# Last part of a Perceiver block on one core: tile 0's steps set between tile 1's, roots by ScalarE's table, and a causal mask added by TensorE

## The chip, the core and the metric

The kernel runs on one core of a Trainium2 chip. A core has TensorE (matrix products into PSUM), VectorE, ScalarE (elementwise functions from a loaded table) and GpSimd, and queues that start DMAs (SyncE's, called SP below, and ScalarE's own). The profile calls them PE (PEld for its weight loads), DVE, ACT, POOL and SP. PSUM has eight banks of 128 x 512 f32. The metric is the device time of one execution, in microseconds; a measurement is the median of several runs.

## What is computed

Everything is float32. Four batches of 256 tokens of width 256 go through three layers; the context of each batch is 4096 tokens of width 192.

```python
x1 = x + xattn(layernorm(x), ctx)      # 16 heads of 16, softmax over 4096 context tokens
x2 = x1 + attn(layernorm(x1))          # causal; q and k normed per head, then scaled
x  = x2 + ffn(layernorm(x2))           # 64 slots: routing, gates, slot attention
# ffn: logits = gelu([x, slot_mean] @ w1 + b1) @ w2 + b2, over |tau| + 0.1
#      alpha  = softmax over the 8 largest of 64, else 0
#      slots  = GRU(alpha^T x / sum alpha, slot_init); slots attend to each other; layernorm
#      out    = alpha @ (slots @ wvp + bvp) @ wo + bo
```

## The kernel before

**The main loop.** For every batch, pairs of 128 context tokens are taken in 16 steps: scores (L165), exp on ScalarE (L1778, L1780), products with the values (L179), sums kept in SBUF by VectorE (L1794). What follows the cross attention of batch b (its output, self attention and feed forward) is cut into small steps, and a dictionary places them between the steps of batch b+1. On TensorE, VectorE and ScalarE the instructions stand in the order in which the program issues them (`manual_schedule`); a step that waits holds all that is behind it on its engine.

**The last batch.** Nothing follows batch 3, so its 256 queries are split into two tiles of 128 (t = 0, 1) at the end: tile 0's cross attention is finished first, and `tile_out` and `tile_in` (L2133, L2156) take tile 0 up to its scaled q and k while tile 1's last context tokens are still being scored. `ending` (L2174) does the rest: both tiles' self attention, the feed forward of batches 2 and 3 together (`both_`, 64 slots each), and the output of all four batches. The eight banks are named x_0, x_1, y_0, y_1, z_0, z_1, w_0, w_1, in pairs x_, y, z, w. Temporaries come from a ring of eight buffers (`temp`).

Names that the prediction uses:

- `tile_qk`, `tile_heads`, `tile_factors` (L1987, L2015, L2021): q and k of a tile in one product, their squares (ScalarE, `Square`), the sum of squares per head (VectorE, L2017), and q and k scaled by one over the root (L2022). `tile_in` finds that root on VectorE alone: `rsqrt` (L925) with a first guess and three Newton rounds of three instructions (L935 to L941). In `ending`, tile 1 uses ScalarE's Sqrt (L2227, L2232) and a reciprocal.
- `preload` (L944) runs a function on one element, so that ScalarE loads its table there.
- `tile_qk_turned` (L2029): q and k transposed by TensorE and moved with gain and bias.
- `first_scores`, `first_weigh` (L2060, L2080): tile 0's queries against tile 0's keys, 16 heads in eight products, exp, and the products with the values. A product of 32 rows uses one of four row strips of TensorE; which one is set by `pair_rows(h, m)`.
- `second_scores`, `second_exp`, `second_mask`, `second_weigh` (L2094 to L2114): the same for tile 1's queries against both tiles' keys, for c = 0, 1 and h = 0, 1; the mask multiplies the part of tile 1's own keys by the triangle `tri` (`tile_mask`, L2053).
- `fill` (L1055): products of zeros into an unused bank, 0.43 us each by its constant.
- `project`, `residual`, `tile_stats`, `normed`: output projection onto the residual in PSUM, its mean and variance, and the normed rows x2n.
- `chosen` (L1433): routing; the largest eight logits, two exps on ScalarE (L1446), alpha (L1448 to L1452). `slot_inputs` (L1456), `gates` (L1494), `slot_qk`, `slot_scores`, `slot_v`, `at_turned`, `mixed_channels_first` (L1600), `slot_values`: the slots' part.
- `given_out` (L1660): the output of one batch, two products with the identity that bring in x2, two with alpha, a copy by ScalarE, and a DMA on SP. Before, batch 0's stands behind the gates, batch 1's behind `at_turned`; batches 2 and 3 are sent last, one on SP and one on ScalarE's queue.

## Time and profile before

| | us |
|---|---|
| median of 3 runs | 851.98 (850.6 to 852.13) |
| the profiled execution | 850.88 |
| its span (first to last instruction) | 849.1 |
| `ending` starts (last products with the context's values, L1900) | 786.2 |
| last product of TensorE ends | 842.07 |
| last two output DMAs are issued | 842.76 and 842.93 |

The page's busy table gives each engine's time at work and its share of the span; the table by stage does the same for stretches of the span. The chain of waits is followed back from the last instruction: at each step to what released it. In the timeline a row is start, length, engine, line, operation, output and inputs, count, and in brackets how long the engine had been idle and who ended that. A product in f32 stands as two records, a transpose as one. Between the last product and the end of the span lie 7 us: the last copies, their DMAs, and the program's end.

### The profile page before, as it was taken

What the parts mean: (1) busy time and instruction counts of PE and PEld (TensorE: products, weight loads), DVE (VectorE), ACT (ScalarE), POOL (GpSimd) and SP (SyncE); (2) the same over time, 40 slices, a digit from 0 to 9 for tenths busy, and PEclk for the clock granted to TensorE, in tenths of its full rate; (3) what the DMA queues carried; (4) which work ended last, traced back from release to release, by engine and by line L of the source; (5) the groups of instructions that cost most, each with busy time, mean ns of one, the idle gap of its engine ahead of it and who ended that gap; (6) DMA issues with size and microseconds to landing.
All of it is one profiled execution on the core that took longest, in us unless ns stands there. A gap on an engine that the chain in (4) does not pass through costs nothing.

```text
span 849.1 us, 19377 instructions
## 1 busy us (share of the span) xinstructions
PE 826.4 (97%) x8403; PEld 451.4 (53%) x8403; DVE 307.3 (36%) x776; ACT 606.0 (71%) x841; POOL 16.8 (2%) x20
## 2 busy tenths in 40 slices
PE   8999999999999999999999999999999999999886
PEld 5445555545555545545545555554545554567564
DVE  3123234222263353212253353232344442113654
ACT  5776776767677768777778777766778777777542
POOL 1000100000000010000000010000000000000000
PEclk9999999999999999999999999999999999999999
DMA  7601001000000000000000000000000000000001
GB/s 205 138 27 50 26 22 55 27 26 25 26 26 26 2 26 26 26 25 27 27 25 26 2 26 26 26 25 10 19 25 26 27 25 25 2 3 2 2 1 54
DMA packets 21822, 25.86 MB, mean 30 GB/s; under 512 B 6241, under 2 KB 13281, under 8 KB 21729
## 3 DMA queue, kind: packets, MB, share of 16 engines
q1 hardware_dynamic: 20784, 23.75, 9.6%
q8 instruction: 68, 1.11, 0.5%
q10 hardware_dynamic: 848, 0.79, 0.3%
q14 instruction: 26, 0.21, 0.1%
q0 software_dynamic: 96, 0.01, 0.0%
HBM read 23.48 MB, written 1.05 MB: 29 GB/s over the span
## 4 chain that ended last, share of the span: by engine, by line
PE 93%; DVE 3%; ACT 2%; issue 1%; DVEq 0%; ACTq 0%
PE banks L165 28%; PE banks L179 25%; PE banks L993 7%; PE banks L80 7%; PE banks L107 7%; PE banks L86 4%; PE banks L120 4%; PE banks L1876 2%; PE banks L1900 1%; PE banks L981 1%; PE banks L1843 1%; PE banks L1058 1%; PE banks L1812 1%; PE banks L194 1%; ACT prob L1780 1%; PE banks L1461 1%
## 5 line engine op out<-in xcount | busy, mean ns | idle before, releaser
L1780 ACT ACTIVATE prob<-banks 128x1024 f32<-128x1024 f32 x360 | 343.8, 1043 | 0.0
L165 PE MATMUL banks<-qh,kt 32*128 32x512 f32 x1920 | 250.2, 620 | 1.2 <-DVE qh L1036 1.2
L179 PE MATMUL banks<-prob,v 128*32 128x256 f32 x3840 | 219.6, 381 | 0.8 <-ACT prob L1822 0.5
L1778 ACT ACTIVATE prob<-banks 128x512 f32<-128x512 f32 x240 | 130.3, 595 | 121.7 <-PE banks L165 121.4
L179 PEld LDWEIGHTS banks<-prob,v 128*32 128x32 f32 x3840 | 118.6, 110 | 117.0 <-ACT prob L1778 42.8
L165 PEld LDWEIGHTS banks<-qh,kt 32*128 32x128 f32 x1920 | 97.6, 183 | 111.1 <-issue 62.5
L1794 DVE TENSOR_TENSOR sums<-banks,sums 128x512 f32<-128x512 f32 x112 | 77.1, 691 | 178.4 <-PE banks L179 155.8
L107 PE MATMUL banks<-wv,ctx 128*128 128x256 f32 x256 | 61.6, 384 | 0.0
L80 PE MATMUL banks<-ctx,wk 128*128 128x512 f32 x128 | 61.5, 603 | 0.1
L107 PEld LDWEIGHTS banks<-wv,ctx 128*128 128x128 f32 x256 | 46.8, 190 | 14.2 <-ACT prob L1778 6.8
L150 DVE COPY v<-banks 128x512 f32<-128x512 f32 x35 | 23.9, 691 | 81.6 <-PE banks L120 77.2
L94 DVE TENSOR_SCALAR kt<-banks,bk 128x512 f32<-128x512 f32 x32 | 24.0, 751 | 66.9 <-PE banks L86 66.8
L150 ACT COPY v<-banks 128x512 f32<-128x512 f32 x29 | 17.0, 587 | 30.0 <-PE banks L120 28.8
L120 PE MATMUL banks<-wv,ctx 64*128 64x256 f32 x256 | 36.3, 402 | 0.0
L86 PE MATMUL banks<-ctx,wk 64*128 64x512 f32 x128 | 36.1, 641 | 0.0
L95 ACT ACTIVATE kt<-banks,bk 128x512 f32<-128x512 f32 x32 | 22.1, 690 | 17.9 <-PE banks L86 17.1
L80 PEld LDWEIGHTS banks<-ctx,wk 128*128 128x128 f32 x128 | 20.9, 189 | 21.2 <-ACT prob L1780 12.1
L120 PEld LDWEIGHTS banks<-wv,ctx 64*128 64x128 f32 x256 | 22.0, 186 | 11.1 <-issue 9.3
L1822 ACT ACTIVATE prob<-banks 128x512 f32<-128x512 f32 (+1 forms) x30 | 17.9, 693 | 8.5 <-PE banks L1812 8.5
L987 DVE COPY tmp<-banks 128x512 f32<-128x512 f32 x17 | 11.8, 691 | 32.8 <-PE banks L981 32.8
L1890 ACT ACTIVATE prob<-banks 128x1024 f32<-128x1024 f32 x24 | 22.9, 1043 | 0.0
L993 PE MATMUL banks<-wqkv,tmp 128*128 128x256 f32 (+1 forms) x56 | 19.6, 482 | 0.5 <-ACT prob L1822 0.5
(310 smaller groups left out, 601.4 us busy)
## 6 DMA issues: line engine op xcount, KB each, us to landing
ctx<-in_ctxT SPq DMA_DIRECT2D x32, 256.0 KB, 3.0
ctx<-in_ctxT SPq DMA_DIRECT2D x64, 128.0 KB, 3.2
x<-in_x SPq DMA_DIRECT2D x4, 256.0 KB, 3.3
wih<-in_ffn_WihT SPq DMA_DIRECT2D x1, 768.0 KB, 7.1
tmp<-in_ffn_WhhT SPq DMA_DIRECT2D x3, 256.0 KB, 4.1
out<-tmp SPq DMA_DIRECT2D x3, 256.0 KB, 2.4
wq<-in_L_xattn_Wq ACTq DMA_DIRECT2D x1, 256.0 KB, 5.6
wo<-in_L_xattn_Wo SPq DMA_DIRECT2D x1, 256.0 KB, 4.7
```

The costliest lines, as they stand in the source:

```text
L80: nc.tensor.matmul(pk[c], k.wk[:, 0, c * P : (c + 1) * P], cx[:, 0, :], start=True, stop=False)
L86: nc.tensor.matmul(pk[c], k.wk[left(c), 1, c * P : (c + 1) * P], cx[left(c), 1, :], start=False, stop=True,)
L94: nc.vector.tensor_scalar(kt[:, 0, :], pk[0], k.bk[:, 0:1], None, ALU.add)
L107: nc.tensor.matmul(pv[n // 2][:, n % 2, :], cx[:, 0, n * P : (n + 1) * P], k.wv[:, 0, :], start=(n % 2 == 0), stop=False, skip_group_check ...
L120: nc.tensor.matmul(pv[u][:, i, :], cx[left(u), 1, n * P : (n + 1) * P], k.wv[left(u), 1, :], start=False, stop=True, skip_group_check=True,)
L150: copy(v[:, :, 0 : H * VW].rearrange("p i (h w) -> p i h w", w=VW)[:, :, :, 0:D], src.rearrange("p i (h d) -> p i h d", d=D),)
L165: nc.tensor.matmul(sc[:, m, :], kt[r, c, i * P : (i + 1) * P], qh[r, c, :], start=True, stop=True)
L179: nc.tensor.matmul(po[q * 32 : (q + 1) * 32, s * NQ : (s + 1) * NQ], v[:, i, w0 : w0 + 32], pr[s][:, m, e * NQ : (e + 1) * NQ], start=(fir ...
L993: nc.tensor.matmul(dst, lhs(c), rhs(c), start=(c == 0), stop=(c == 1))
L1778: nc.scalar.activation(pt[:, m, :], sc[:, m, :], AF.Exp)
L1780: nc.scalar.activation(pt, sc, AF.Exp)
L1794: nc.vector.tensor_tensor(s.sums[c], bank, s.sums[c], ALU.add)
```

## The change

- **Set-up**: a second constant, `hidden_by`, is made from the triangle `tri`: 0 where a key is visible, -2^100 where it is hidden.
- **`tile_in`**: alpha's transposes go to another bank and their copy later; the root of tile 0 is taken as tile 1's (`tile_roots`: ScalarE's Sqrt, then a reciprocal), with an Exp preload behind it.
- **`ending`, first half**: tile 0's transposes, moves, first scores, exps and weighing are cut by half (`tile_turned`, `tile_moved`, `first_scores(s, pair, c, h)`, `first_weigh(s, pr, g, bank)`) and set between tile 1's steps. The second scores are issued by (c, h), own keys first. In two of the four cases (bank pair y) TensorE first writes `ident @ hidden_by` into the part of the own keys, and the scores are added to it; these have no multiplication by VectorE. The other two keep theirs.
- **`ending`, second half**: the fills are gone; `tile_stats` and the roots come in another order; Gelu, Exp and Sqrt are preloaded; `given_out` is split into `residual_out` (the two products that bring in x2) and the rest; batch 0's output goes ahead of the routing's exps and batch 1's ahead of `slot_qk`.

Helpers not shown are the old ones cut in two (`tile_stats` and `tile_variance` return their second half, `tile_weigh` takes the blocks it is to do, `tile_v` the halves). The core of the diff:

```diff
@@ -1139,6 +1141,9 @@
         nc.vector.tensor_scalar(tri, bank[:, 0:P], 0.0, None, ALU.is_ge)
+        nc.vector.tensor_scalar(
+            hidden_by, tri, 2.0**100, -(2.0**100), ALU.mult, ALU.add
+        )
         for v in vself:
...
+        var = s.var_t[:, t, :]
+        rs = small.tile([P, 2 * H + 1], F32, name="rs_t", tag="rs_t", bufs=1)
+        nc.scalar.activation(rs[:, 2 * H :], var[:, 2 * H :], AF.Sqrt)
         nc.vector.tensor_reduce(
-            s.var_t[:, t, 0 : 2 * H], sq.rearrange("p (h d) -> p h d", d=D), AX.X, ALU.add
-        )
+            var[:, 0 : 2 * H], sq.rearrange("p (h d) -> p h d", d=D), AX.X, ALU.add
+        )
+        nc.vector.tensor_scalar(var[:, 0 : 2 * H], var[:, 0 : 2 * H], BIG, None, ALU.min)
+        nc.scalar.activation(
+            rs[:, 0 : 2 * H],
+            var[:, 0 : 2 * H],
+            AF.Sqrt,
+            bias=s.eps_t[:, t : t + 1],
+            scale=1.0 / D,
+        )
+        return rs
...
-    def first_scores(s, pairs):
-        prs = []
+    def first_scores(s, pair, c, h):
+        for m in range(2):
+            r = pair_rows(h, m)
+            nc.tensor.matmul(
+                pair[:, m, c * NQ : (c + 1) * NQ],
+                s.sk[r, c, 0:P],
...
+    def second_hidden(pair):
         for m in range(2):
             nc.tensor.matmul(
+                pair[:, m, NQ : 2 * NQ],
+                ident,
+                hidden_by.unsqueeze(1).to_broadcast([P, 2, P]),
                 start=True,
+                stop=False,
+                skip_group_check=True,
+            )
+    def second_scores(s, c, h, pair, add=False):
+        for j in (1, 0):
+            for m in range(2):
+                r = pair_rows(h, m)
+                nc.tensor.matmul(
+                    pair[:, m, j * NQ : (j + 1) * NQ],
+                    s.sk[r, c, j * P : (j + 1) * P],
+                    s.sq[r, c, :, P:],
+                    start=not (add and j == 1),
+                    stop=True,
+                    skip_group_check=add,
+                )
...
@@ -2158,18 +2199,18 @@
         s, d = batches[B - 1], batches[B - 2]
         s.x1T = halves(temp())
         tokens_turned(x_0, s.xo, 0)
+        move = alpha_turned(d, x_1, True)
         tokens(s.x1T, x_0, 0, nc.vector.tensor_copy)
-        alpha_turned(d, y_1)
         s.qk = held.tile([P, QT, 2 * C], F32, name="qk", tag="qk", bufs=1)
         s.sq = held.tile([P, 2, 2, NQ], F32, name="sq", tag="sq", bufs=1)
         s.sk = held.tile([P, 2, NQ], F32, name="sk", tag="sk", bufs=1)
-        sq = tile_qk(s, 0, x_1)
+        sq = tile_qk(s, 0, x_0)
         tile_v(s, 0, y_0)
-        tile_heads(s, 0, sq)
-        heads_ = s.var_t[:, 0, 0 : 2 * H]
-        nc.vector.tensor_scalar(heads_, heads_, 1.0 / D, s.eps_t[:, 0:1], ALU.mult, ALU.add)
-        s.rs0 = rsqrt(s.var_t[:, 0, :])
-        tile_factors(s, 0, x_1, s.rs0[:, 0 : 2 * H])
+        move()
+        s.rs0 = tile_roots(s, 0, sq)
+        preload(AF.Exp)
+        nc.vector.reciprocal(s.rs0, s.rs0)
+        tile_factors(s, 0, x_0, s.rs0[:, 0 : 2 * H])
...
         tile_add(s, 0, y_1, 1)
-        tile_weigh(blocks, 1, x_0)
-        tile_add(s, 1, x_0, 1)
-        tile_qk_turned(s, 0, z_0, z_1, act, act, act)
-        tile_v_moved(s, 0, y_0, s.rs0[:, 2 * H :])
-        for c, bank in enumerate((w_0, w_1)):
-            tile_turn(tile_of(s.sums[c], 1), bank)
+        tile_weigh(blocks, 1, x_1, (0,))
+        tile_turned(s, 0, 0, z_0)
+        tile_weigh(blocks, 1, x_1, (1,))
+        tile_add(s, 1, x_1, 1)
+        for i in range(2):
+            tile_moved(s, 0, i, z_0, act)
+        tile_turn(tile_of(s.sums[0], 1), w_0)
+        tile_turned(s, 0, 1, z_1)
+        tile_moved(s, 0, 4, z_1, act)
+        tile_turn(tile_of(s.sums[1], 1), w_1)
         puts = [tile_divide(s, bank, (c,), 0, 1) for c, bank in enumerate((w_0, w_1))]
         tokens_turned(y_1, s.att, 1)
         tokens(s.attT, y_1, 1, vec.tensor_copy)
         for put in puts:
             put(vec.tensor_copy)
-        prs = first_scores(s, (z, w))
+        tile_v_moved(s, 0, y_0, s.rs0[:, 2 * H :])
+        first_scores(s, z, 0, 0)
+        first_scores(s, z, 1, 0)
+        f0 = second_exp(z)
         project(s, wo, x_0, 1)
         tile_residual(s, x_0, 1)
+        first_scores(s, w, 0, 1)
+        tokens_turned(y_1, s.xo, 1)
+        var = tile_variance(s, 1)
+        tokens(s.x1T, y_1, 1, vec.tensor_copy)
+        var()
+        first_scores(s, w, 1, 1)
+        f1 = second_exp(w)
         preload(AF.Sqrt)
-        tokens_turned(y_1, s.xo, 1)
-        tokens(s.x1T, y_1, 1, vec.tensor_copy)
-        tile_mask(prs[0].rearrange("p m (u q) -> p m u q", q=P))
-        tile_variance(s, 1)
         sq = tile_qk(s, 1, x_1)
-        tile_mask(prs[1].rearrange("p m (u q) -> p m u q", q=P))
-        tile_v(s, 1, x_0)
-        var = s.var_t[:, 1, :]
-        rs = small.tile([P, 2 * H + 1], F32, name="rs_t", tag="rs_t", bufs=1)
-        act.activation(rs[:, 2 * H :], var[:, 2 * H :], AF.Sqrt)
-        tile_heads(s, 1, sq)
-        nc.vector.tensor_scalar(
-            var[:, 0 : 2 * H], var[:, 0 : 2 * H], BIG, None, ALU.min
-        )
-        act.activation(
-            rs[:, 0 : 2 * H], var[:, 0 : 2 * H], AF.Sqrt, bias=s.eps_t[:, 1:2], scale=1.0 / D
-        )
-        nc.vector.reciprocal(rs, rs)
+        for pt in (f0, f1):
+            tile_mask(pt.rearrange("p m (u q) -> p m u q", q=P))
+        first_weigh(s, f0, 0, z_0)
+        tile_v(s, 1, x_0, (0,))
+        first_weigh(s, f1, 1, z_0)
+        tile_v(s, 1, x_0, (1,))
+        rs = tile_roots(s, 1, sq)
+        sums0 = op.tile([P, 2 * NQ], F32, name="sums", tag="sums")
+        vec.tensor_copy(sums0[:, 0:C], z_0[:, 0:C])
+        act.copy(sums0[:, C:], z_0[:, C:])
+        sums0 = sums0.rearrange("p (g q) -> p g q", q=P)
+        preload(AF.Exp)
+        vec.reciprocal(rs, rs)
         tile_factors(s, 1, x_1, rs[:, 0 : 2 * H])
-        first_weigh(s, prs, z_0)
-        sums0 = as_sums(z_0, 4, act.copy)
-        preload(AF.Exp)
+        second_hidden(y)
         for c in range(2):
             tile_turn(sums0[:, 2 * c : 2 * c + 2, :], z_1, c)
-        fill(w_0, 0.86)
-        tile_qk_turned(s, 1, y_0, y_1, vec, vec, act)
+        for i, bank in enumerate((w_0, w_1)):
+            tile_turned(s, 1, i, bank)
+        tile_moved(s, 1, 0, w_0, vec)
+        tile_moved(s, 1, 1, w_0, vec)
+        tile_moved(s, 1, 4, w_1, act)
         tile_v_moved(s, 1, x_0, rs[:, 2 * H :])
         s.att, s.attT = halves(temp()), halves(temp())
         put = tile_divide(s, z_1, (0, 1), 1, 0)
         put(vec.tensor_copy)
-        for j in range(2):
-            for h, pair in enumerate((x_, y)):
-                second_scores(s, 0, h, pair, j)
-        p0 = [second_exp(pair) for pair in (x_, y)]
-        tokens_turned(w_0, s.att, 0)
         with_abo(0)
-        tokens(s.attT, w_0, 0, vec.tensor_copy)
-        residual(0, w_1)
-        second_mask(p0[0])
-        p1 = []
-        for h, pair in enumerate((x_, y)):
-            for j in range(2):
-                second_scores(s, 1, h, pair, j)
-            p1.append(second_exp(pair))
-        project(s, awo, w_1, 0, alone=False)
-        second_mask(p0[1])
-        mv0 = tile_stats(w_1[:, 0:C])
+        second_scores(s, 0, 0, y, True)
+        p00 = second_exp(y)
+        second_scores(s, 0, 1, w)
+        p01 = second_exp(w)
+        tokens_turned(x_1, s.att, 0)
+        tokens(s.attT, x_1, 0, vec.tensor_copy)
+        with_abo(1)
+        residual(0, x_0)
+        second_scores(s, 1, 0, z)
+        p10 = second_exp(z)
+        second_hidden(y)
+        second_scores(s, 1, 1, y, True)
+        p11 = second_exp(y)
+        preload(AF.Sqrt)
+        second_mask(p01)
+        second_weigh(s, p00, 0, 0, w_0)
+        second_weigh(s, p01, 0, 1, w_0)
+        second_mask(p10)
+        sums0 = as_sums(w_0, 2, vec.tensor_copy)
+        project(s, awo, x_0, 0, (0,), alone=False)
+        second_weigh(s, p10, 1, 0, w_1)
+        second_weigh(s, p11, 1, 1, w_1)
+        tile_turn(sums0, z_0)
+        sums1 = as_sums(w_1, 2, vec.tensor_copy)
+        residual(1, w_0)
+        put0 = tile_divide(s, z_0, (0,), 1, 1)
+        tile_turn(sums1, z_1)
+        project(s, awo, x_0, 0, (1,), alone=False)
+        tokens_turned(y_0, s.att, 1, (0,))
+        tokens(s.attT, y_0, 1, act.copy, (0,))
+        put1 = tile_divide(s, z_1, (1,), 1, 1)
+        tokens_turned(y_1, s.att, 1, (1,))
+        mv0 = tile_stats(x_0[:, 0:C])
+        tokens(s.attT, y_1, 1, act.copy, (1,))
+        project(s, awo, w_0, 1, alone=False)
         rs2 = small.tile([P, 2], F32, name="rs2_t", tag="rs2_t", bufs=1)
-        nc.vector.tensor_scalar(rs2[:, 0:1], mv0[:, 1:2], EPS, BIG, ALU.add, ALU.min)
-        with_abo(1)
-        second_weigh(s, p0, 0, z_0)
-        sums0 = as_sums(z_0, 2, vec.tensor_copy)
-        second_mask(p1[0])
-        preload(AF.Sqrt)
-        residual(1, w_0)
-        act.activation(rs2[:, 0:1], rs2[:, 0:1], AF.Sqrt)
-        second_mask(p1[1])
-        second_weigh(s, p1, 1, z_1)
-        sums1 = as_sums(z_1, 2, vec.tensor_copy)
-        tile_turn(sums0, x_0)
-        put0 = tile_divide(s, x_0, (0,), 1, 1)
-        tile_turn(sums1, y_0)
-        tokens_turned(x_1, s.att, 1, (0,))
-        tokens(s.attT, x_1, 1, act.copy, (0,))
-        put1 = tile_divide(s, y_0, (1,), 1, 1)
-        tokens_turned(y_1, s.att, 1, (1,))
-        project(s, awo, w_0, 1, (0,), alone=False)
-        tokens(s.attT, y_1, 1, act.copy, (1,))
-        nc.vector.reciprocal(rs2[:, 0:1], rs2[:, 0:1])
...
+        def root(t, mv):
+            nc.vector.tensor_scalar(rs2[:, t : t + 1], mv[:, 1:2], EPS, BIG, ALU.add, ALU.min)
+            act.activation(rs2[:, t : t + 1], rs2[:, t : t + 1], AF.Sqrt)
+            nc.vector.reciprocal(rs2[:, t : t + 1], rs2[:, t : t + 1])
...
-        normed(0, w_1, mv0)
-        project(s, awo, w_0, 1, (1,), alone=False)
-        act.copy(s.x2[:, 0, :], w_1[:, 0:C])
+        root(0, mv0)
+        normed(0, x_0, mv0)
         mv1 = tile_stats(w_0[:, 0:C])
+        root(1, mv1)
...
+        tokens_turned(x_1, s.x2n, 0)
+        tokens(s.x2nT, x_1, 0, act.copy)
+        residual_out(batches[0], y_0)
         normed(1, w_0, mv1)
...
-        gelu0 = hidden_product(0, x_1)
-        fill(y_1, 0.43)
-        tokens_turned(z_1, s.x2n, 1)
+        gelu0 = hidden_product(0, w_1)
+        tokens_turned(z_0, s.x2n, 1)
+        preload(AF.Gelu)
         gelu0()
-        tokens(s.x2nT, z_1, 1, vec.tensor_copy)
+        tokens(s.x2nT, z_0, 1, vec.tensor_copy)
+        logits(s, 0, x_1[:, 0:SLOTS])
+        gelu1 = hidden_product(1, z_1)
+        gelu1()
+        preload(AF.Exp)
+        act.copy(s.x2[:, 0, :], x_0[:, 0:C])
         act.copy(s.x2[:, 1, :], w_0[:, 0:C])
-        hidden_product(1, w_1)()
-        with_bias(s, "x2", s.x2, fbo)
         put0(vec.tensor_copy)
         put1(vec.tensor_copy)
-        logits(s, 0, x_0[:, 0:SLOTS])
-        fill(y_1, 0.43)
-        logits(s, 1, y_0[:, 0:SLOTS])
         lg = small.tile([P, QT, SLOTS], F32, name="lg", tag="lg", bufs=1)
-        for t, bank in enumerate((x_0, y_0)):
+        logits(s, 1, y_1[:, 0:SLOTS])
+        for t, bank in enumerate((x_1, y_1)):
             nc.vector.tensor_tensor(lg[:, t, :], bank[:, 0:SLOTS], b2, ALU.add)
         route = chosen(s, lg)
         next(route)
-        slot_inputs(d, z_0, z_1)
-        fill(x_1, 0.86)
+        slot_inputs(d, w_1, z_0)
+        given_out(batches[0], y_0)
         finish(route)
-        slot_inputs(s, y_1, w_0)
-        alpha_turned(s, w_1)
-        finish(gates(both_, x_1, z_1, y_0))
+        with_bias(s, "x2", s.x2, fbo)
+        slot_inputs(s, z_1, x_1)
+        alpha_turned(s, w_0)
+        finish(gates(both_, w_1, z_0, y_1))
         check_range = all_in_range()
         next(check_range)
-        given_out(batches[0], x_0)
-        slot_qk(both_, y_1, w_0)()
-        mixing = slot_scores(both_, w_1)
+        residual_out(batches[1], x_0)
+        given_out(batches[1], x_0)
+        slot_qk(both_, z_1, x_1)()
+        mixing = slot_scores(both_, w_0)
...
-        move = slot_v(both_, x_1)
+        move = slot_v(both_, y_0)
         finish(mixing)
+        preload(AF.Sqrt)
         move()
-        kept_slots(both_, z_1)
-        at_turned(both_, y_1)
...
-        for t in range(QT):
-            nc.tensor.matmul(
-                w_1[:, t * C : (t + 1) * C], ident, d.x2[:, t, :], start=(t == 0), stop=False,
+        residual_out(d, x_1)
...
```

## Prediction

> **What bounds the kernel now.** The page's busy table and 40 slices come first, then the table by stage, with columns start:stop, length, then busy time (and count) of TensorE, its weight loads, VectorE, ScalarE and GpSimd, granted clock, DMA share, GB/s.

> ```profile
> span 849.1 us, 19377 instructions
> PE 826.4 (97%) x8403; PEld 451.4 (53%) x8403; DVE 307.3 (36%) x776; ACT 606.0 (71%) x841; POOL 16.8 (2%) x20
> ...
> 790.00:800.00 10.00, 8.36 (x52) 4.80 (x56) 6.29 (x19) 5.96 (x10) 0.00 (x0) 1.00 0.00 0
> 800.00:810.00 10.00, 7.89 (x84) 5.48 (x86) 5.57 (x14) 7.18 (x11) 0.00 (x0) 1.00 0.01 2
> 810.00:820.00 10.00, 7.51 (x91) 4.78 (x84) 6.54 (x22) 4.76 (x11) 0.51 (x1) 1.00 0.01 2
> ```

> Up to some 780 us TensorE is never idle, and the change leaves that order alone. What can move is the last 65 us, where no engine is full and the end hangs on a chain of handovers. So I read the chain of waits (start, length, what held it) from 785 us on:

> ```profile
> 789.35 0.70 DVE qk L2022
> ...
> 798.70 1.13 DVE prob L2053
> ...
> 802.18 0.86 PE banks L1058 x4
> ...
> 811.42 1.21 DVE prob L2053 x2
> ...
> 835.81 0.87 PE banks L1664 x4
> 836.67 1.06 PE banks L1646 x4
> ```

> Here stand the things the change touches: the factors of tile 0 (L2022), which end ten small VectorE steps of a root (L935 to L941); masks L2053; `fill` products L1058; the output of batch 1 (L1664, L1646) ahead of the slots' mixing.

> The timeline gives the prices:

> ```profile
> 804.51 1.15 PE L2098 MATMUL banks<-sq,sk 32*128 32x256 f32 x16 [1.02 <-DVE rect L1934]
> 807.68 0.73 PEld L2098 LDWEIGHTS banks<-sq,sk 32*128 32x128 f32 x8 [0.18 <-ACT prob L2108]
> 795.75 1.28 ACT L946 ACT_TABLE_LOAD   x1
> 797.04 0.20 ACT L946 ACTIVATE preload<-ones 1x1 f32<-1x1 f32 x1
> 831.33 0.59 ACT L1670 COPY tmp<-banks 128x512 f32<-128x512 f32 x1 [0.80 <-PE banks L1646]
> 837.78 0.71 PE L1600 MATMUL banks<-atT,fv 128*128 128x128 f32 x4
> ```

> One product is two records. Sixteen records over four row strips take 1.15 us; eight that use only two strips still load for 0.73 us, as long as the sixteen (0.74 at 804.50). So scores issued by one half (h) alone run two at a time: 0.85 us for four products.

> **The sum.** I laid the new order out engine by engine: each step starts at its engine's previous end or, if later, 0.03 us (0.05 on TensorE) after what it waits for, with durations from these rows. Below, "old" is the trace, and differences are new minus old.

> *Tile 0's roots.* Old: `alpha_turned` writes y_1 and waits until 782.78 for an exp that reads that pair; the q,k product follows at 783.41. New: it writes x_1, free at 781.86, so q,k starts at 782.50 and the Square is held only by the last exp (784.61): it ends at 785.22, not 786.03. Then, new on ScalarE: alphaT's copy 0.37, a table load 1.28, two roots 0.20 and 0.32, to 787.35 (VectorE's reduce 0.68 and min 0.19 lie beside). Reciprocal 0.36, factors 0.69: 788.46 against 790.04. The ten steps removed took 787.06 to 789.32. Little of this 1.6 reaches the end at once: three quarters of the weighing must pass TensorE first (to 788), the last quarter follows, so the second turning of sums starts only 0.5 earlier and the tokens are copied at 792.3 against 792.83. The added Exp load (1.28) and preload (0.20) lie beside the transposes; uncovered they would cost 1.5.

> *Projection of tile 1.* Old: after all eight `first_scores` products, which also waited for the dens copies: end 795.21. New: only four go before (0.85 instead of 1.79 from the same point): 0.5 + 0.9 gives -1.4. Residual, transposes, tokens and q,k keep this lead (q,k ends 797.3 against 798.67).

> *Roots of tile 1.* Square waits for the Sqrt preload at 797.7, not TensorE, and keeps -1.0; but both masks (2 x 1.22) now precede the reduce instead of holding it (798.70 in the chain), and the factors end at 800.6 against 802.13: -1.5. The q,k transposes no longer stand behind two fill products (0.86): scores can start at 802.25 against 804.51, -2.25.

> *Second scores and masks.* Two mask summands of two products each are added: 4 x 0.43 = 1.7 us of TensorE. The first pair lies beside the roots. The second waits for the exp of the bank (804.5) and is on the path: with two-strip scores the last exp ends at 808.55 against 809.88, so 0.9 of the lead is given back. But its bank now needs no mask: old, VectorE had statistics, a bias add, a copy and two masks (2 x 0.65) after it, and the weighing ended at 813.08; new, the weighing follows that exp directly and ends at 810.0: -3.1. Division, projection, statistics, root and norm (same rows) keep -3.0: 815.0 against 817.99.

> *Routing.* The Gelu preload holds logits 0 until 816.2, and these hold the second hidden product: -2.8 at the logits (818.45 against 821.27). Then a wait is added. On ScalarE the two exps of the routing now stand behind `given_out` of batch 0, whose copy (0.59) waits for `slot_inputs` (1.5) and two 64-row products (1.13) on TensorE: 820.5. The exps end at 821.7; VectorE, done with the other inputs at 820.3, waits 1.4, and behind it alpha, the inputs and the gates. Lead here: -1.45, kept to snT (830.4 against 831.97).

> *Mixing.* L1600 stood behind batch 1's output, 835.64 to 837.73, while atT was ready at 836.14: 1.6 lost. The output now goes before `slot_qk`, beside the gates. Lead -3.3, and -3.4 at the last product (838.7 against 842.07).

> The DMAs of batches 0 and 1 go out earlier on SP (old 831.94 and 838.4), each landing some 2.4 us later with nothing else in that queue; the last two are unchanged. GpSimd's bias add starts at 819.6 as before (819.49), with 19 us to spare. The new VectorE step that makes the mask (128x128; nearest row L1141, 0.28) lies in the first 70 us.

> Laying out the *old* order in the same way ends 0.5 us before its trace, nearly all in the last 15 us, so I take like with like: -3.0. Bounds come from the price of changing the shape of products on TensorE, which no row isolates: at 0 the difference is -3.5, at 0.2 us it is -2.1; I take 0.1, which fits the old trace best. The profiled execution was 850.88 (span 849.1), giving 847.9. That is 1.1 below the median of the runs, 851.98, so the forecast against the median is 849.0.

> [...] The table-load rows show the next instruction 0.01 us after 1.28: no more. [...]

> For the clock:

> ```profile
> 844.00:845.00 1.00, 0.00 (x0) 0.00 (x0) 0.00 (x0) 0.00 (x0) 0.00 (x0) 1.00 0.97 323
> 845.00:846.00 1.00, 0.00 (x0) 0.00 (x0) 0.00 (x0) 0.00 (x0) 0.00 (x0) 0.55 0.36 122
> 846.00:847.00 1.00, 0.00 (x0) 0.00 (x0) 0.00 (x0) 0.00 (x0) 0.00 (x0) 0.50 0.10 25
> ```

> The clock halves 3.0 us after the last product. The change removes every fill in this part, and my layout has one gap of 2.4 us (820.5 to 822.9); the old order's longest is 1.2. [...]

> **Rivals.**
> *The lead is eaten on the way (about 851, no change).* ScalarE now carries two more loads and more waits; if the wait before the routing's exps is 1 us longer and the two-strip scores 1 us dearer, -1.0 remains: 851.0. For: -1.45 is all that is left at the gates in my sum. Against: the -1.9 after it is a removed queue, not a race.
> *The clock halves in the 2.4 us gap (slower, about 855.5).* After it the chain holds 6.6 us of products (0.66 inputs, 1.2 gates, 1.1 and 0.33 of q,k and scores, 0.33, 0.71, 1.13, 1.14). Half speed to the end costs +6.6: 849.0 + 6.6 = 855.6; one stretch as long as the 3.4 us up to the first gates costs 2 and ends within no change. It is slower from 4.7 us of doubled products on. For: 3.0 us of idleness did it, and nothing fills the gaps any more. Against: 2.4 is less.
> *More is won (847.3).* If the exps get through before batch 0's output, the 1.4 returns; only the written order of ScalarE speaks against it, firmly.

> **Numbers.** Forecast 0.64, eaten 0.18, clock 0.12, more 0.06. 0.2% (1.7 us) is what a measurement here can tell: faster is below 850.3. The forecast's own bounds (-3.5 to -2.1, and 1 us of spread between runs) are 847.5 to 850.9, mostly faster: with "more", 0.66. Same: 0.22. Slower: 0.12. The range reaches down for "more" and up through "eaten" to 852.8, leaving out most of the clock.

> **What would show it.** In the new profile: factors of tile 0 some 1.6 earlier; last second exp to weighing with no VectorE between; ScalarE's copy for batch 0's output just ahead of the routing's exps, with VectorE idle about 1.4 before L1453; TensorE idle 2.4 there, clock 1.00; L1606 directly after atT. A clock of 0.5 before the last product, or table loads that hold the next instruction longer than 1.3, would make it wrong.

## The result and the profile after

| | before | changed |
|---|---|---|
| median of 4 runs | 851.64 us (850.60 to 852.13) | 4627.69 us (4624.19 to 4629.42) |
| ratio | | 5.434, 95% interval 5.425 to 5.444 |
| span of the profiled execution | 849.1 | 4627.6 |
| instructions in it | 19377 | 47480 |
| the four outputs are all issued by | 842.93 | 845.11 |

The kernel takes five times as long, and not in the part that was changed. The page of the changed kernel, its first lines and two of its costliest groups (group, count, then busy time and mean ns):

```profile
span 4627.6 us, 47480 instructions
PE 3430.5 (74%) x18909; PEld 1338.5 (29%) x18909; DVE 3585.2 (77%) x3999; ACT 1836.0 (40%) x2308; POOL 161.3 (3%) x94
...
L406 ACT ACTIVATE gprob<-gprob 128x1024 f32<-128x1024 f32 x512 | 540.7, 1057 | 679.2 <-DVE gprob L403 507.1
L378 DVE TENSOR_TENSOR top<-top,raw 128x1024 f32<-128x1024 f32 x512 | 623.6, 1218 | 70.9 <-ACT raw L377 70.9
```

L362 to L406 do not run at all in the kernel before. They belong to `exact`, a second path that stands in both kernels and that no line of the diff touches. Behind the outputs stands a test: `all_in_range` compares every softmax denominator kept in the tile `dens` with 1e-10 and 1e15, `count_bad` counts the rows that fail, and a branch runs `exact` if there is one:

```python
    redo = fast(tc, a, out, k, const, x0)
    with tc.If(redo > 0):
        exact(tc, a, out, k)
```

The chain of waits of the changed kernel (start, length, what held it) shows the branch being taken:

```profile
844.39 0.70 DVE tmp L2437
845.55 0.82 ACTq L2543
846.65 6.22 DMA g_x<-in_x
...
881.33 1.23 DVE top L378
882.55 1.13 DVE ne L379
```

L2437 is the last step of the output, L2543 hands the count of the test to the queues, and right behind it x is loaded again as `g_x`. From there to the end all four batches are computed a second time.

What made the test fail is in the timeline of the changed kernel. `dens` gets batch 3's self-attention denominators by two small copies, L1955 (`put0` and `put1`, which `tile_divide` returns):

```profile
816.62 0.41 PE L1959 MATMUL banks<-ident,x2n 128*128 128x128 f32 x2
817.06 0.42 DVE L1965 COPY tmp<-banks 128x256 f32<-128x256 f32 x1 [0.53 <-PE banks L1959]
817.41 0.15 DVE L1955 COPY dens<-banks 128x8 f32<-128x8 f32 x1
...
818.11 0.66 PE L993 MATMUL banks<-tmp,w 128*128 128x128 f32 x4
...
819.21 0.17 DVE L1955 COPY dens<-banks 128x8 f32<-128x8 f32 x1 [1.65 <-ACT hT L2372]
```

The trace calls every bank `banks`; the code says which. `put0` reads z_0 and `put1` reads z_1. In the new order `tokens_turned(z_0, s.x2n, 1)` writes z_0 at 816.62 and `hidden_product(1, z_1)` writes z_1 at 818.11, both ahead of the copies. The trace even puts the second copy's wait down to ScalarE's Gelu (L2372), which reads that hidden product and has nothing to do with denominators. So `dens` holds elements of x2n and of the hidden layer. No view shows the values; a row of x2n has mean zero, so some should be negative, below the test's 1e-10. Before, put0 and put1 read x_0 and y_0, which nothing writes until the logits (L1417), and these come behind both copies:

```profile
819.26 0.23 DVE L1942 COPY dens<-banks 128x8 f32<-128x8 f32 x2
...
819.95 0.33 PE L1417 MATMUL banks<-w,hT 128*128 128x64 f32 x2
```

In the part that was changed, the outputs are 2.2 us later than before too, where the forecast had them 3 us earlier. Of these 2.2, 1.04 had come up in the main loop of that execution; 1.1 are left. The same chain there:

```profile
806.65 1.06 PE banks L2124 x4
...
822.10 0.59 ACT tmp L1682
822.68 0.49 ACT tmp L1451 x2
824.39 2.82 PE banks L1466 x12
```

The second mask summand (L2124) holds the last scores; the copy of batch 0's output (L1682) holds the routing's exps (L1451); and the second slot inputs (L1466) take 2.82 us, against 1.55 at full clock (824.10 to 825.65 in the kernel gap_filled, below). VectorE's wait for the exps (L1453) and TensorE's gap behind it stand in the timeline:

```profile
823.20 0.29 DVE L1453 SCALAR_TENSOR_TENSOR lg<-tmp 128x128 f32<-128x128 f32 x1 [1.31 <-ACT tmp L1451]
...
824.39 1.12 PE L1466 MATMUL banks<-alpha,sumto 128*128 128x64 f32 x4 [2.33 <-DVE alpha L1457]
```

The table by stage (start:stop, length, busy us of TensorE, its loads, VectorE, ScalarE, GpSimd, clock, DMA share, GB/s) shows the clock of these slow products:

```profile
816.28:819.69 3.41, 2.14 (x16) 1.72 (x16) 1.05 (x5) 2.35 (x5) 0.00 (x0) 1.00 0.00 0
819.69:823.11 3.42, 2.37 (x16) 1.84 (x15) 2.01 (x11) 2.52 (x7) 1.26 (x1) 1.00 0.00 0
823.11:826.52 3.41, 2.13 (x10) 2.13 (x11) 1.82 (x6) 0.06 (x1) 0.00 (x0) 0.50 0.21 77
```

The granted clock is 0.50 from 823.11 to 829.93 and again from 836.76 to 840.17, for 6.83 and 3.41 us. The first fall comes 1.05 us into TensorE's gap of 2.33 (822.06 to 824.39), not behind it.

### The profile page after: what moved, and what is told of

Same layout as the page of the kernel before. It is cut to its first block, busy times and chain, and to the rows that moved or that the text cites. A ratio compares the mean times of both kernels' runs of the same rounds, so it can differ in the third digit from the quotient of the medians.

```text
span 4627.6 us, 47480 instructions
## 1 busy us (share of the span) xinstructions
PE 3430.5 (74%) x18909; PEld 1338.5 (29%) x18909; DVE 3585.2 (77%) x3999; ACT 1836.0 (40%) x2308; POOL 161.3 (3%) x94
## 4 chain that ended last, share of the span: by engine, by line
DVE 49%; PE 37%; ACT 6%; issue 3%; POOL 3%; DMA 1%; SPq 0%; ACTq 0%; DVEq 0%; POOLq 0%
DVE top L378 12%; DVE ne L379 12%; DVE nan L380 12%; PE ring L165 7%; DVE gprob L402 6%; PE banks L165 5%; ACT gprob L406 5%; PE banks L179 5%; DVE gprob L403 3%; PE po L179 3%; PE ring L80 2%; POOL shift L383 2%; PE ring L86 1%; PE ring L107 1%; PE banks L993 1%
## 5 line engine op out<-in xcount | busy, mean ns | idle before, releaser
L165 PE MATMUL ring<-qh,kt 32*128 32x512 f32 x4096 | 1530.2, 995 | 729.2 <-ACT raw L377 505.0
L377 ACT COPY raw<-ring 128x1024 f32<-128x1024 f32 x512 | 515.1, 1012 | 1093.4 <-DVE ne L379 1046.9
L165 PEld LDWEIGHTS ring<-qh,kt 32*128 32x128 f32 x4096 | 424.9, 268 | 1645.4 <-ACT raw L377 1167.6
L406 ACT ACTIVATE gprob<-gprob 128x1024 f32<-128x1024 f32 x512 | 540.7, 1057 | 679.2 <-DVE gprob L403 507.1
L378 DVE TENSOR_TENSOR top<-top,raw 128x1024 f32<-128x1024 f32 x512 | 623.6, 1218 | 70.9 <-ACT raw L377 70.9
L379 DVE TENSOR_TENSOR ne<-raw 128x1024 f32<-128x1024 f32 x512 | 623.5, 1218 | 0.0
L380 DVE TENSOR_TENSOR nan<-nan,ne 128x1024 f32<-128x1024 f32 x512 | 623.3, 1217 | 0.0
L402 DVE TENSOR_SCALAR gprob<-ring 128x1024 f32<-128x1024 f32 x512 | 603.6, 1215 | 14.5 <-PE ring L165 14.2
L403 DVE TENSOR_TENSOR gprob<-gprob,shift 128x1024 f32<-128x1024 f32 x512 | 604.5, 1216 | 2.0
L179 PE MATMUL po<-gprob,g_v 128*32 128x256 f32 x4096 | 399.5, 469 | 233.3 <-ACT gprob L406 228.7
```

What stands on the lines that cost most here:

```text
L165: nc.tensor.matmul(sc[:, m, :], kt[r, c, i * P : (i + 1) * P], qh[r, c, :], start=True, stop=True)
L179: nc.tensor.matmul(po[q * 32 : (q + 1) * 32, s * NQ : (s + 1) * NQ], v[:, i, w0 : w0 + 32], pr[s][:, m, e * NQ : (e + 1) * NQ], start=(fir ...
L377: nc.scalar.copy(raw, sc)
L378: nc.vector.tensor_tensor(half, half, raw, ALU.max)
L379: nc.vector.tensor_tensor(ne, raw, raw, ALU.not_equal)
L380: nc.vector.tensor_tensor(nan, nan, ne, ALU.max)
```

## The experiments

Each kernel was measured beside runs of the kernel before on the same chip, whose medians were 851.20 to 851.58.

### What runs the second path

Theory A: the late copies. Theory B: the summand of -2^100 makes denominators out of range.

**puts_early**, the copies ahead of the rewriting:

```diff
         normed(0, x_0, mv0)
+        put0(vec.tensor_copy)
+        put1(vec.tensor_copy)
         mv1 = tile_stats(w_0[:, 0:C])
...
-        put0(vec.tensor_copy)
-        put1(vec.tensor_copy)
```

> The changed kernel with one edit: the two copies of batch 3's self-attention denominators (put0, put1) go behind the norm of tile 0, ahead of the products that rewrite banks z_0 and z_1. Theory A (late copies: the range test reads x2n's transposes and the hidden products, finds them out of range, and the kernel runs its second path, exact): the second path does not run, the page has no lines of exact behind the outputs, and the time is that of the fast part alone. Its last output DMA was issued at 845.11 in the changed kernel's profile against 842.93 before, so 851.6 + 2.2 = 853.8 us, between 852.5 and 855.5. Theory B (the mask summand of -2^100 makes denominators that fail the range test): nothing changes, 4620 to 4635 us. With 2.33 us of idle TensorE ahead of the second slot inputs left in place, the granted clock falls to 0.50 there again.

Measured: 851.91 us (850.88 to 854.48, 12 runs), ratio 1.0002 (0.9993 to 1.0011): no second path, as theory A has it, though the median lies below the 852.5 to 855.5 expected. The trace of puts_early has both copies ahead of the transposes, and nothing behind the last output:

```profile
814.87 0.23 DVE L1955 COPY dens<-banks 128x8 f32<-128x8 f32 x2
...
816.94 0.41 PE L1959 MATMUL banks<-ident,x2n 128*128 128x128 f32 x2
...
846.44 0.40 ACTq L1662 DMA_DIRECT2D out<-tmp  x1
```

**before_rewritten**, the kernel before with the fault alone:

```diff
-        tokens_turned(z_1, s.x2n, 1)
+        tokens_turned(x_0, s.x2n, 1)
...
-        tokens(s.x2nT, z_1, 1, vec.tensor_copy)
+        tokens(s.x2nT, x_0, 1, vec.tensor_copy)
```

> The kernel before with one edit: the transposes of x2n of tile 1 go to bank x_0, which holds batch 3's denominators until put0 has copied them, and no other bank; masks, roots and order stay. Theory A: x2n has negative values, so the range test fails and the second path runs: 851.6 + some 3776 (4627.7 less 851.6) = about 4625 us, 4615 to 4635. Theory B: there is no summand, so the second path does not run: 850.5 to 852.5 us.

Measured: 4625.1 us, one run. The timeline of before_rewritten: copy of tokens, then of `dens`, and behind the outputs `exact` starts:

```profile
819.39 0.42 DVE L1952 COPY tmp<-banks 128x256 f32<-128x256 f32 x1 [0.94 <-PE banks L1946]
819.74 0.23 DVE L1942 COPY dens<-banks 128x8 f32<-128x8 f32 x2
...
844.04 0.91 DVE L362 MEMSET nan<- 128x1024 f32 x1 [0.68 <-DVE tmp L2388]
```

**masks_multiplied**, the changed kernel with the copies late and no summand:

```diff
-        second_hidden(y)
...
-        second_scores(s, 0, 0, y, True)
+        second_scores(s, 0, 0, y)
...
+        second_mask(p00)
         second_mask(p01)
         second_mask(p10)
+        second_mask(p11)
```

> The changed kernel without the summand: the four banks of second scores are masked by VectorE's multiplication as before, and the copies of the denominators stay late. Theory A: 4620 to 4635 us. Theory B: the range test passes, the second path does not run, 850 to 857 us.

Measured: 4623.14 us, one run. Theory A holds in all three and B in none: the copies alone, in either kernel, switch 3.77 ms on and off.

### The clock

puts_early is the change without its fault, and it is as fast as before. Its 12 executions go from 850.9 to 854.5, at mean clocks of 0.995 down to 0.991; before's stand mostly at 0.998. **gap_filled** is puts_early with zeros in the gap:

```diff
         given_out(batches[0], y_0)
+        fill(y_1, 1.72)
         finish(route)
```

> puts_early with four products of zeros (some 1.7 us) behind batch 0's output products, in the gap of 2.33 us ahead of the second slot inputs. Theory C (the lead is lost to the clock, which halves because of this gap): granted clock 1.00 from 820 to 833, the stretch from alpha's end to snT takes 7.7 us as before and not 10.2, and the time is 2.5 us under puts_early, 3.5 if the second fall at 837 goes too: about 850.5, 849.5 to 851.5. Theory D (the clock falls for another reason, or the lead was lost in the order of the handovers): 853.8, within 0.7 us of puts_early.

Measured: 849.11 (848.20 to 853.40, 12 runs); 0.9986 (0.9970 to 1.0002), just below the 849.5 to 851.5 expected. Eight executions lie at 848.2 to 849.6 (clock 0.997 to 0.999), four at 853.1 to 853.4 (0.991, 0.992). In the profiled one, windows as long as those above stay at full clock:

```profile
815.38:818.80 3.42, 2.21 (x14) 1.46 (x12) 1.36 (x4) 2.37 (x6) 0.00 (x0) 1.00 0.00 0
818.80:822.21 3.41, 3.27 (x20) 2.79 (x21) 2.02 (x11) 2.49 (x6) 1.22 (x1) 1.00 0.00 0
822.21:825.62 3.41, 3.00 (x20) 2.40 (x18) 1.81 (x6) 0.67 (x3) 0.04 (x1) 1.00 0.21 77
```

Theory C holds where the clock does, but the gap is not all of it.

**fills_back** adds two products to gap_filled (`fill(y_1, 0.43)` behind `tokens_turned(z_0, s.x2n, 1)`, `fill(w_1, 0.43)` ahead of the second `logits`):

> gap_filled with two more products of zeros where the kernel before had them: behind x2n's second transposes and ahead of the second logits. In gap_filled 4 of 12 executions still took 853.1 to 853.4 at a mean clock of 0.991, the others 848.2 to 849.6 at 0.997 to 0.999. Theory C1 (the clock falls after any stretch of some 3.4 us in which TensorE works for less than two thirds, wherever the throttle's own period happens to begin; the changed order has such a stretch at 816 to 820 too): no execution above 850.5, median 848.6. Theory C2 (the falls in gap_filled come from elsewhere, or are chance of the chip): a third of the executions stay at 853, the median where it was, 849.1.

Measured: 848.67 (848.16 to 849.06, 5 runs); 0.9959 (0.9943 to 0.9975). No execution fell (mean clocks 0.997 to 0.999), as C1 expected. Five are few, though: if a third of them still fell, five in a row would hold about once in eight.

**copy_behind** is puts_early with batch 0's output behind the routing's exps:

```diff
+        finish(route)
         given_out(batches[0], y_0)
-        finish(route)
```

> puts_early with batch 0's output (its products, its copy by ScalarE, its DMA) issued behind the routing's two exps, and no fill. The order on TensorE is the same; on ScalarE the exps no longer stand behind the copy. VectorE's wait ahead of L1453 (1.31 us in the changed kernel) goes, so alpha ends 1.3 earlier and TensorE's gap of 2.33 becomes 1.0. Where the clock holds: gap_filled's undisturbed 848.5 less 1.3 = 847.2. By C1 the stretch at 816 to 820 is still under two thirds, so some executions fall and come out 3 to 5 higher: lowest 846.9, highest over 850, median 847 to 850. By the theory that only the gap of 2.33 matters, all lie within 1 us of 847.2.

Measured: 849.56 (848.51 to 852.32, 12 runs); 0.9977 (0.9964 to 0.9989). Six executions at 848.5 to 848.7 with a clock of 0.997, six at 850.4 to 852.3 with 0.989 to 0.994: as C1 has it, the clock still falls in half of them. The undisturbed ones are 1.3 above the 847.2 expected, no faster than those of gap_filled; in the profiled one alpha came 0.8 earlier than in fills_back (counted from the last scores of the context), not 1.3. The wait ahead of L1453 is gone, but L1453 itself is shown with 0.86 us there, against 0.29 in the changed kernel and in fills_back; why stays open:

```profile
821.38 0.86 DVE L1453 SCALAR_TENSOR_TENSOR lg<-tmp 128x128 f32<-128x128 f32 x1
```

**before_no_fills**, the kernel before without its four `fill` lines:

> The kernel before without its four fills (six products of zeros, 2.6 us by their constant) in the last part. If fills cost what the chain shows and nothing else, the fill ahead of tile 1's transposes (0.86 on the path) comes free: 851.5 - 0.9 = 850.6. If they hold the clock (C1), most executions lose it at 816 to 824, where TensorE is then busy for half the time: 3 to 4 us more, median 853 to 855, with a mean clock of 0.991 to 0.993.

Measured: 853.63 (851.35 to 856.47, 12 runs); 1.0020 (1.0007 to 1.0034), mean clock 0.986 to 0.996. In this run the fills of zeros, of which one stands on the path, are worth 2 us to the kernel before.

**routing_first** is puts_early with two fills as in fills_back, and:

```diff
+        finish(route)
         slot_inputs(d, w_1, z_0)
         given_out(batches[0], y_0)
-        finish(route)
...
         normed(0, x_0, mv0)
+        act.copy(s.x2[:, 0, :], x_0[:, 0:C])
         mv1 = tile_stats(w_0[:, 0:C])
+        act.copy(s.x2[:, 1, :], w_0[:, 0:C])
         root(1, mv1)
```

> puts_early with the routing finished first: the exps and alpha's four VectorE steps go ahead of batch 2's slot inputs on VectorE (1.1 us of work) and of batch 0's copy on ScalarE, the two copies of x2 by ScalarE go ahead of tile 1's root, and two products of zeros stand where the kernel before had them (as in fills_back); none in the gap, which closes. Exps from 820.4 instead of 822.3, alpha's end 822.0 instead of 824.0 (gap_filled's times): -2.0, of which 0.2 is lost as TensorE reaches the second slot inputs at 821.8 at the earliest. Expected 848.5 - 1.8 = 846.7 us, 845.8 to 847.8, under both kernels; if the clock falls all the same, 850 and more.

Measured: 847.50 (846.79 to 849.63, 5 runs); 0.9945 (0.9929 to 0.9961). Alpha ends 2.0 earlier than in fills_back, as expected. But in the profiled execution the clock fell right there:

```profile
818.93:822.35 3.42, 3.07 (x21) 2.54 (x21) 2.32 (x14) 2.48 (x5) 0.00 (x0) 1.00 0.00 0
822.35:825.76 3.41, 3.41 (x17) 2.96 (x16) 1.71 (x5) 0.06 (x1) 0.00 (x0) 0.50 0.22 77
```

TensorE was busy for 3.07 of 3.42 us, and its longest pause was 0.33. So this fall came without a long gap and without little busy time, and C1's two thirds do not hold for it. The window is full of products of 64 columns or 64 rows. I counted the work: in gap_filled's trace the records of the fills (128 rows x 256 columns) start 0.216 us apart, so a window holds 16 of them; each record counts by its columns and rows against that, and one that lies across two windows is shared out by time. By this count the window above comes to 0.36, although it is 0.90 busy.

**routing_filled** adds one `fill(y_1, 0.43)` behind `given_out(batches[0], y_0)`:

> routing_first with one product of zeros more, ahead of the second slot inputs. In routing_first's profile the clock fell at 822.35 though TensorE was busy for 90% of the window that ended there: counted by rows and columns of its products it did 0.36 of what 128 x 256 products would do, and in all traces so far windows under 0.37 were followed by a fall, windows from 0.38 on were not. The product adds 0.12: the window comes to 0.45, no execution falls, and the time is 846.9 in all of them, 846.4 to 847.7. If busy time or luck decides and not the counted work: again about two in five at 847.5 to 849.6.

Measured: 846.33 (846.11 to 847.72, 6 runs); 0.9931 (0.9904 to 0.9958). The counted work of the profiled window at 820.63 is 0.56, and the clock holds. One execution of six has 0.996, the others 0.998 to 0.999.

### What the parts are worth

Three parts undone, each against fills_back (848.67).

**masks_back**: the four masks by VectorE, the edit of masks_multiplied.

> fills_back without the summand: the four banks are masked by VectorE's multiplication. By the prediction's sum the summand costs 0.9 of the lead (two products of 0.43 on the path) and frees the weighing from 1.8 us of VectorE work behind the last exp, so this kernel is 0.9 slower than fills_back (848.67): 849.6. Rival: the order of the scores brought that gain and not the summand; then the exp ends 0.45 earlier, the mask of 0.65 stands behind it, and the time is within 0.4 of fills_back.

Measured: 847.26 (846.67 to 848.44, 9 runs); 0.9943 (0.9923 to 0.9963). Not 0.9 slower: 1.4 faster (on another chip, where the kernel before took 851.58 against 851.57 beside fills_back). TensorE and ScalarE in fills_back:

```profile
806.37 1.13 PE L2124 MATMUL banks<-hidden_by,ident 128*128 128x256 f32 x4
807.43 1.13 PE L2138 MATMUL banks<-sq,sk 32*128 32x256 f32 x8
...
808.61 1.02 ACT L2149 ACTIVATE prob<-banks 128x1024 f32<-128x1024 f32 x1 [1.10 <-PE banks L2138]
```

and ScalarE, VectorE and TensorE in masks_back:

```profile
804.08 3.84 ACT L2149 ACTIVATE prob<-banks 128x1024 f32<-128x1024 f32 x4 [1.17 <-PE banks L2138]
...
807.95 0.69 DVE L2088 TENSOR_TENSOR prob<-prob,tri 128x512 f32<-128x512 f32 x1 [0.22 <-ACT prob L2149]
...
807.85 1.27 PE L2160 MATMUL banks<-prob,vself 128*32 128x128 f32 x32
```

Without the summand the four exps run without a pause; each mask (0.69) lies beside the next exp (they follow each other every 0.96), and only the last one stands behind its exp. With it ScalarE stands 1.10 ahead of the last exp. From the last scores of the context to alpha it is 42.31 us, against 43.89 in fills_back.

**one_summand**: only the second summand gone, p11 masked by VectorE.

> fills_back with the summand in the first bank only; the fourth bank is masked by VectorE. In fills_back's trace the second summand (1.13 us of records at 806.37) holds the last scores, and ScalarE stands idle for 1.10 ahead of the last exp; the first lies at 800.41, where TensorE otherwise waits for the factors. If the price of 1.4 us that masks_back showed is the second summand's alone: 847.3, as masks_back, within 0.5. If the first one costs too (products of another shape just ahead of the transposes, or its bank): half way, 848.0 or more. If it pays (one VectorE multiplication less): 846.8 or less.

Measured: 846.55 (846.48 to 848.12, 5 runs); 0.9950 (0.9937 to 0.9964). To alpha it is 42.30, as in masks_back: in these traces the whole price is the second summand's, and the first, beside the roots, is free. That one_summand's median is 0.7 below masks_back's is less than either's spread.

**batch1_late**: batch 1's output back behind `at_turned`.

> fills_back with batch 1's output (four products, copy, DMA) back behind at_turned, as in the kernel before. By the prediction's sum that output then holds L1606 up by some 1.9 us: 850.6. By C1 it also takes dense work out of the window at 829 to 832.5 (about half of its counted work), so the clock may fall there in some executions: those would be 2 to 3 us longer still, 852 to 854. If the move brought nothing: 848.7.

Measured: 853.18 (852.48 to 853.77, 12 runs); 1.0009 (0.9994 to 1.0024). 4.5 slower, and in every execution, with a clock of 0.993 to 0.995. Table by stage, then TensorE and VectorE, of batch1_late:

```profile
828.87:832.28 3.41, 0.75 (x8) 0.60 (x7) 3.05 (x10) 0.75 (x2) 0.00 (x0) 1.00 0.00 0
832.28:835.70 3.42, 2.89 (x13) 2.13 (x12) 1.88 (x8) 1.64 (x4) 0.00 (x0) 0.50 0.02 5
```

```profile
836.97 1.91 PE L1669 MATMUL banks<-x,ident 128*128 128x256 f32 x4
838.81 1.26 PE L1652 MATMUL banks<-sv,alphaT 64*128 64x256 f32 x4
...
840.12 0.71 PE L1606 MATMUL banks<-atT,fv 128*128 128x128 f32 x4
...
837.21 0.29 DVE L1591 COPY atT<-banks 128x128 f32<-128x128 f32 x1 [0.64 <-PE banks L1589]
```

atT is there at 837.50 and L1606 starts at 840.12: 2.6 us behind the output, part of it slow (L1669 took 1.91 us there, 1.03 at full clock in gap_filled). In its new place the output fills the one long pause of TensorE (0.75 us busy of the 3.41 from 828.87 above), while the gates are worked out by VectorE.

**roots_back**: tile 0's root by `rsqrt`'s ten VectorE steps, no Sqrt and Exp load there.

> fills_back with tile 0's root by VectorE's Newton steps again (ten small instructions, 2.26 us) and without ScalarE's Sqrt and Exp loads there. By the prediction's sum the factors of tile 0 end 1.6 later and little of it, 0.5 us, reaches the end: 849.2. If the quicker root carries the lead: 850.3. If the table loads cost as much as they save: 848.7 or less.

Measured: 849.88 (849.10 to 850.36, 12 runs); 0.9967 (0.9950 to 0.9984): 1.2 slower, not 0.5. Counted from the last scores of the context, the factors of tile 0 end at 9.59 against 8.68 in fills_back, 0.91 later and not 1.6, and alpha is 0.97 later: what the root itself is worth arrives whole. The rest of the lead at the factors (1.81 in all against the kernel before) is there without the table's root: alpha's transposes go to another bank, and the 0.90 us that TensorE stood idle ahead of them before (at 782.83) are gone.

**routing_masks**, routing_filled without the summands:

> routing_filled with all four banks masked by VectorE, no summand. If the two gains lie on one chain one after the other (weighing, then routing), they add: 846.33 - 1.41 = 844.9, 844.3 to 845.8. If the earlier weighing only moves a wait ahead of the routing: 846.0 or more. The counted work of the window at 827.5 to 831 was 0.37 in routing_filled, at the edge; where a window comes out lower the clock falls and the time is 2 to 3 us more in that execution.

Measured: 844.74 (844.47 to 845.43, 5 runs); 0.9923 (0.9909 to 0.9937). The two gains add, and this version is faster than both kernels.

## Why the prediction was wrong

The step that failed is the sentence "What can move is the last 65 us". The prediction took the instructions of the kernel before and put them in a new order; it never asked which of the moved ones decide that other instructions run at all. put0 and put1 are in the diff, renamed banks and all, and the prediction does not name them: two copies of 0.15 us off the path. What matters of them is not their price but what they read, and when. No rival had a kernel that takes its second path, and no range would have held it. puts_early, before_rewritten and masks_multiplied show that this, and not the summand, is the 3.77 ms.

For the rest, the traces can be laid side by side from a common point, the start of the last scores of the context (779.55 before, 780.59 in the changed kernel: its main loop reached that point 1.04 later). In us from there, with gap_filled as the change without fault and with its clock:

| | before | predicted | changed | gap_filled |
|---|---|---|---|---|
| factors of tile 0 end | 10.49 | 8.91 | 8.68 | 8.68 |
| factors of tile 1 end | 22.58 | 21.05 | 21.36 | 21.37 |
| norm of tile 1 ends | 38.44 | 35.45 | 35.94 | 36.09 |
| alpha ends | 44.75 | 43.30 | 43.75 | 43.89 |
| snT ends | 52.42 | 50.85 | 53.96 | 51.56 |
| last product ends | 62.52 | 59.15 | 63.65 | 60.07 |

- *Roots of tile 0, projection, roots of tile 1, second scores.* Right to 0.35 us (second scores 23.03 after that point, 22.70 predicted). The price of 0.1 us for a change of product shape, which the sum takes and has its bounds from, was the author's fit to the trace of the kernel before; no run isolates it. But the sum's "Little of this 1.6 reaches the end at once" failed: of the 1.8 measured at the factors, the root's own share is 0.91, and all of it arrives (0.97 at alpha, 1.2 in the median of roots_back), not 0.5.
- *Masks.* The lead at the norm was there (2.5 of 3.0), for another reason. The sum gave it to the bank that "now needs no mask"; masks_back shows the new order has it without the summand and 1.4 us more. The sum compared the new order with summand to the old order without, where statistics and a bias add stood between the masks; the new order without summand was not laid out.
- *Routing.* The wait was there: 1.31 at L1453 for 1.4. Lead at alpha 1.0 for 1.45.
- *Clock.* The rival that had 0.12 happened: "The clock halves in the 2.4 us gap". The gap was 2.33, but only 1.05 of it lay ahead of the fall, so its full length cannot be the reason; and the clock was lost twice. What it cost: to the last output DMA 64.52 in the changed kernel, 60.93 in fills_back, 3.6 us; the rival's bounds were 2 and 6.6. That the clock holds over the gap of 2.4 us, which the sum takes for granted, no trace of the kernel before showed. "Against: 2.4 is less" failed: it compared gaps, and in these traces the falls went with the work counted in a window (0.30 from 819.69 to 823.11, ahead of the first).
- *Mixing.* L1606 did follow atT directly (at 839.78; the copy of atT ends at 839.73). batch1_late puts the move at 4.5, not 1.9 (of which the sum names 1.6 for the wait and leaves the rest without a term): the output's old place cost the wait (atT at 837.50, L1606 at 840.12), and with its new place the clock held too (mean 0.997 to 0.999 in fills_back, 0.993 to 0.995 in batch1_late).
- *Table loads and gaps.* The table loads held nothing longer than the sum had it: in the changed kernel too, preloads (L946) follow their loads of 1.28 us at once, 0.02 us behind the load at 797.56. The length of a gap did not tell whether the clock holds: it fell 1.05 us into a gap (changed kernel) and behind a window whose longest pause was 0.33 (routing_first).

Rows of the changed kernel behind the last two points:

```profile
797.56 1.28 ACT L946 ACT_TABLE_LOAD   x1
798.86 0.20 ACT L946 ACTIVATE preload<-ones 1x1 f32<-1x1 f32 x1
...
839.44 0.29 DVE L1591 COPY atT<-banks 128x128 f32<-128x128 f32 x1 [0.64 <-PE banks L1589]
...
839.78 0.89 PE L1606 MATMUL banks<-atT,fv 128*128 128x128 f32 x4 [0.26 <-DVE nbad L1701]
```

Without the fault and with fills the change is worth 2.9 us (851.57 to 848.67; by the ratio 3.5, 2.1 to 4.9). The sum had 3.0 (its own 3.4 less 0.5 would be 2.9) and 849.0. That it agrees is partly luck: the roots and batch 1's output brought more than it said, the summand took 1.4 away, and the fills, with which the clock held (mean 0.997 to 0.999 in fills_back, 0.991 to 0.995 in puts_early), were not in the change: without them and without the fault it is no faster than before (puts_early, 851.91).

## What to carry to other kernels

When steps are reordered by hand and banks are renamed, go through every reader of every bank whose writers moved, above all the cheap readers whose result only steers something: a guard that reads too late leaves the outputs right and runs the fallback. Where a fast path has a fallback, the instruction count of the profile is the first number to look at. Before fills are taken out, or dense products moved, look at the granted clock of the trace and count the work of TensorE between its changes (here in windows of 3.41 us) by rows and columns, not its busy time: here the clock fell behind a window that was 0.90 busy and counted 0.36 (routing_first), and held behind one that was 0.56 busy and counted 0.38 (the kernel before). Products of an output that is not urgent can go where that count is low; those of batch 1's output were worth 4.5 us there (batch1_late).
